# A decoder layer on one core: the values of two entries made by seven block products, with a new order of the slot

## The chip, the cores and the metric

The kernel runs on one core of a Trainium2 chip. The metric is the device time of one execution in microseconds (us), as the median of several runs.

## The reference, cut to what matters

One decoder layer on x of 16 entries, 128 tokens, 256 features, all float32: self attention with 16 heads of 64, cross attention with 16 heads of 16 to a context of the same size, and a feed-forward part of 8 experts with 512 hidden units each, all of them summed for every token. Each part adds to x after a layer norm. The change concerns the values of the self attention and their use:

```python
Q = jnp.einsum('btd,hkd->bthk', x, W_Q) + b_Q
K = jnp.einsum('btd,hkd->bthk', x, W_K) + b_K
V = jnp.einsum('btd,hkd->bthk', x, W_V) + b_V
attn = jax.nn.softmax(scores, axis=-1)
out_h = jnp.einsum('bhqs,bshk->bqhk', attn, V)
```

and the experts' first product, `einsum('nd,edh->neh', xf, w1)`, since a part of it is made early.

## The kernel before

The attention of the 16 entries runs in 16 slots, one for each entry. Slot s holds the self attention of entry s, the first steps of the cross attention of entry s-1 (its queries, scores and softmax) and the last ones of entry s-2, and it prepares later entries. After the slots comes a short tail, and then the experts, for 4 times 512 tokens.

**The order.** PE, DVE, ACT and POOL execute their instructions in the order in which the program gives them. Each step has a name and a due time in a table (DUE; FIRST_DUE and SECOND_DUE replace it for slots 0 and 1). `at` and `due` put a step on a heap at EXTRA + s x SLOT + DUE[name], and the steps are emitted in the order of these times. So only the order counts on the chip; a due time over SLOT falls into the next slot. Names that the prediction uses: S0, S1 (self scores, two halves of eight heads), max/ex/r/mul (softmax: DVE maximum, ACT exponentials of four heads with their sums, DVE reciprocal, POOL scaling; a c ahead means cross), T1 (transposes of the self weights on PE) and T2 (of the cross weights), each with a copy out of PSUM (a name that ends in e), SVa and SVb (self weights times values), SO and CO (output products, with xsSO and xsCO adding to x), bn, bn3 and root (variances and inverse roots of the two layer norms, on DVE), xn, xn3, LNx, LN3, LN1 (normalizing and transposing), CQ, CS, CV, ck, cvr (cross queries, scores, values, keys, value rows), q1x to qc0 and k1x to kc0 (queries and keys of two entries).

**Queries and keys** of a pair of entries are already made with seven block products in place of eight (`paired_steps`): `weight_sums` makes sums of weight blocks in slot 0, `pair_factors` makes four sums of token blocks of a pair (step tf), and each of the seven products is one of them times the other. What the products have in common is added outside PE: ACT copies (u0, c00), DVE adds (u1, u2, u3, c1, c0). One half of the columns of a pair is made in each slot, in four steps on PE (1x, 1y, 2x, 2y), and a later step adds to a PSUM bank that the adds have read before. The sums lie in `places`: sums_q (in a place of its own) and sums_k, which borrows the place w1_1 of a quarter of the experts' weights.

**Values** are made plainly (`values`, L604 on): one entry a slot, two halves of 512 columns, each two matmuls of 128x512 (128 deep, since 256 features are two blocks), and one ACT copy of 128x512 (ve0, ve1).

**Experts' weights ahead of time.** The first matmuls of the experts for tokens 0 to 511 are made already in slots 14 and 15 and in the tail (`pre_hidden`, L921 on; PRE_STEPS says at which step of those slots). Matmuls 0 to 7 need the first quarter of w1 (w1_0), the next eight the second (w1_1). SyncE's queue loads a quarter (1 MB) with one DMA (L242): w1_0 at the start of the kernel, w1_1 at S0 of slot 14, when sums_k is no longer read.

The tail's own PE and ACT instructions keep the order of the program too, but its DVE instructions do not: there the compiler's scheduler orders them by priority, and copies out of PSUM have a high one.

PSUM: scores use two double banks, and everything else in the slots rotates through four banks (`psum_mm`), so the fifth user waits until the first one's copies are done.

```python
a[1][0] = a[0][0] - a[1][0]   # combined(): the fourth of a weight's four sums, in place
nc.tensor.matmul(mm, tokens(b, k), wv[:, k, f], start=(k == 0), stop=(k == KD - 1))   # values
nc.tensor.matmul(mm, w1q[p // (NP // QN)][:, i, k, p % (NP // QN)], xnT[:, k, :MT], ...)   # pre_hidden
```

Of the kernel before, what the change touches and what calls it, by code (L numbers as in the profile page):

```python
# [48 lines left out]
NROW = 528  # L49


SLOT = 27.34
EXTRA = 7.5
DUE = dict(
    S0=0.0, S1=1.0, max0=1.2, LNx=2.0, LN3=2.22, max1=2.34, LNxc=2.42, cvr=2.44, LN3c=2.72,
    tf=3.0, ex0a=3.02, T2b1=3.31, T2b2=3.75, T2b1e=3.94, CQ=4.18, cvre=4.39, T2b2e=4.54,
    ex0b=4.74, T2a1=5.05, r0a=5.14, q2T=5.27, mul0a=5.42, T2a2=5.49, T2a1e=5.69, q1x=5.92,
    ex1a=6.11, T2a2e=6.28, xn1=6.5, q1y=6.82, r0b=6.88, mul0b=7.16, qu0=7.49, r1a=7.69, v1=7.72,
    ex1b=7.99, mul1a=8.19, qu1=8.21, qu2=8.64, qu3=9.07, LN1=9.44, r1b=9.56, ve1=9.64, q2x=9.66,
    st0=9.75, mid=9.77, late=9.77, st1=9.8, mul1b=9.84, LN1c=10.1, q2y=10.11, qc00=10.4,  # L60
    qc1=11.21, CS=11.23, qc0=11.56, msk0=12.38, T1a1=12.4, T1a2=12.84, ab1=13.0, T1a1e=13.03,
    T1b1=13.27, T1a2e=13.53, msk1=13.57, T1b2=13.71, T1b1e=14.03, CV=14.24, T1b2e=14.53,
    cmax0=14.76, SVa=15.29, at2T=15.9, cex0a=16.08, SVb=16.19, cmax1=16.24, CO=17.19,
    atT0=17.38, cex0b=17.45, atT1=17.98, k1x=18.05, cr0a=18.58, xsCO=18.71, cex1a=18.82,
    cmul0a=18.86, k1y=18.95, cr0b=19.05, bn3=19.18, SO=19.85, cmul0b=19.88, ku0=20.2, cr1a=20.4,
    cex1b=20.7, cmul1a=20.9, ku1=20.92, ku2=21.35, mid2=22.0, late2=22.0, ku3=22.03, cr1b=22.38,
    cmul1b=22.9, k2x=23.3, xsSO=23.5, k2y=23.75, bn=23.91, kc00=23.95, root=24.51, ck=24.65,
    v0=25.52, cke=25.72, kc1=26.86, kc0=27.21, ve0=27.44, xn=27.65, xn3=27.98, ab2=28.15,
)


# [9 lines left out]
    q1=17.2, atT1=17.21, q1e=17.6, k1=18.0, w1q=18.1, tf=18.2, SO=19.16, ke1=19.6, ws1=19.7,
    w1k=20.0, xsSO=22.81, bn=23.22, v1=23.47, root=24.79, xn=25.0, ck=25.2, ve1=25.39, q1x=26.9,
    qu0=26.95, cke=27.0, q1y=27.8, qu1=28.2, ab2=28.44, ab1=28.5, k1x=28.7, qu2=28.8, qu3=29.2,
    ku0=29.3, ku1=29.85, q2x=30.5, q2y=30.95, qc00=31.0, k1y=31.85, qc1=32.0, k2x=32.8,
    ku2=32.9, ku3=33.3, kc00=33.3, qc0=33.32, k2y=33.4, kc1=34.5, kc0=34.9,
)

SECOND_DUE = dict(xn1=2.9, ku0=18.7, st2=13.0, st3=22.4)

PRE_STEPS = (  # L90
    (14, "q1x", "qu1"), (14, "k1x", "kc00"),
    (15, "q1x", "qu1"), (15, "v1", "ve1"), (15, "k1x", "kc00"), (15, "v0", "ve0"),
)
ON_ACT = ('T1a', 'T1b')

EARLY = range(2, 6)
LATER = (("mid", range(6, 10), (1,), 2), ("late", range(10, B), (3, 4, 5), 6))
# [3 lines left out]
def decoder_layer(  # L101
# [53 lines left out]
    def psum_mm(name):  # L155
        return ps_mm.tile([P, 512], F32, tag="mm", name=name)
# [83 lines left out]
    def load_w1(i, pool):  # L240
        w = pool.tile([P, KD, E * F // QN], F32, tag=f"w1_{i}", name=f"w1_{i}")
        nc.sync.dma_start(out=w, in_=w1[:, :, i * E * F // QN : (i + 1) * E * F // QN])  # L242
        w1q[i] = w.rearrange("p k (q i c) -> p i k q c", i=2, c=P)

    def load_w2(i, pool):
# [1 line left out]
        nc.sync.dma_start(out=w, in_=w2[:, NF // QN * i : NF // QN * (i + 1), :])  # L247
        w2q[i] = w.rearrange("p (q j) (i c) -> p i j q c", j=2, c=P)

    load_w1(0, we1)  # L250

    places = (
        keep.tile([P, 4 * 512], F32, tag="k3", name="sums_q"),
        we1.tile([P, 4 * 512], F32, tag="w1_1", name="sums_k"),
    )


# [54 lines left out]
    def inverse_root(v, n, parts=None):  # L314

        y = small.tile([P, n], F32, tag=f"root{n}", name="root", bufs=6 if n < 3 else 1)
        t = small.tile([P, n], F32, tag=f"root_t{n}", name="root_t", bufs=2 if n < 3 else 1)
        nc.vector.tensor_scalar(t.bitcast(I32), v.bitcast(I32), 1, None, ALU.arith_shift_right)  # L320
# [23 lines left out]
    def variances(n):  # L344
        return small.tile([P, n, 2], F32, tag=f"mv{n}", name="mv", bufs=6 if n < 3 else 1)

    def statistics(mv, b):
        st = small.tile([P, 6], F32, tag="st", name="st")
# [3 lines left out]
    def inverse_deviations(mv, bs, parts=None):  # L352

        n = len(bs)
        v = small.tile([P, n], F32, tag=f"var{n}", name="var", bufs=6 if n < 3 else 1)
        nc.vector.tensor_scalar_add(v, mv[:, :, 1], LN_EPS)
        r = inverse_root(v, n, parts)
        return {b: (mv[:, i, 0:1], r[:, i : i + 1]) for i, b in enumerate(bs)}
# [172 lines left out]
        paired[x, n] = combined(a, more.rearrange("p (n q c) -> p n q c", n=3, c=P))  # L531

    def pair_factors(b0):
        t = places[b0 // 2 % 2][:, 1536:].rearrange("p (n t) -> p n t", n=4)
        x4 = [[tokens(b0 + i, k) for i in range(2)] for k in range(2)]
        paired[b0] = right(t, x4[0][0], x4[0][1], x4[1][0], x4[1][1])

    def paired_steps(x, b0, n):
# [26 lines left out]
        def first():  # L565
            v["a"], v["b"] = bank()
            product(1, v["a"], clears=True)
            product(6, v["b"])
            u = v["u"] = ap.tile([P, 2, 2, T], F32, tag="su", name="su")
            due(f"{x}u0", with_bias, u[:, 0], v["a"], 1)  # L570
            due(f"{x}u1", nc.vector.tensor_tensor, u[:, 0], u[:, 0], v["b"], ALU.add)

# [30 lines left out]

        return {f"{x}1x": first, f"{x}1y": second, f"{x}2x": third, f"{x}2y": fourth}  # L604

    def values(b, n, name="ve{}"):
        mm = psum_mm("mm_v")
        if ("v", b) not in entry:
            entry["v", b] = ap.tile([P, HD1], F32, tag="v", name="v")
        f = slice(n * 512, (n + 1) * 512)  # L610
        for k in range(KD):
            nc.tensor.matmul(  # L612
                mm,
                tokens(b, k),
                wv[:, k, f],
                start=(k == 0),
                stop=(k == KD - 1),
            )
        due(name.format(n), nc.scalar.copy, entry["v", b][:, f], mm)

    def self_scores(b, half):

# [19 lines left out]
    def self_values(b, half):  # L642


        if half == 0:
            entry["atT", b] = work.tile([P, C1, T], F32, tag="atT", name="atT")
        v, atT, prT = entry["v", b], entry["atT", b], entry["prT", b, half]
        po = psum_mm("po1").rearrange("p (c t) -> p c t", c=4)
        for c in range(4):
            for j in range(2):  # L650
                h = 2 * (4 * half + c) + j
# [31 lines left out]
    def cross_keys(b):  # L683
# [24 lines left out]

        due("cke", out)
        entry["k2T", b] = kT  # L710
        if i == GB - 1 and g + 2 < NG:
            contexts[g + 2] = context(g + 2)

    def cross_value_rows(b):
        g, i = b // GB, b % GB
        mm = psum_mm("mm_v2")
        for k in range(KD):
# [228 lines left out]
    def slot(s):  # L946
# [27 lines left out]
        if bs:  # L974
            at("LN1", self_norm_transposed, bs)
        b0 = s + 2 - s % 2
        if s % 2 == 0 and b0 < B:
            at("tf", pair_factors, b0)
# [470 lines left out]
```

## Time and profile before

| | |
|---|---|
| median of 3 runs | 858.74 us (858.65 to 858.94) |
| the profiled execution's own time | 858.52 us |
| its span, first to last instruction | 856.7 us |
| PE busy in the span | 847.0 us, 99% |
| DVE, ACT, POOL busy | 628.9, 462.3, 163.8 us |
| granted TensorE clock | 0.998 of full speed |
| slots 0 and 1 begin | 12.59 and 48.27 us |
| slots 2, 3, 4 begin | 74.13, 101.05, 128.54 us |
| slots 14, 15, tail begin | 400.90, 425.13, 449.28 us |

A slot is reckoned here from the first matmul of S0 to the next slot's. A busy share says little of PE: the trace models the ends of matmuls, and a matmul's record is longer than the time until the next one starts (593 ns against 430 ns for 128x512). So what an instruction costs PE is read from start to start, and that is done in the prediction. In rows with xN, N instructions in a row are merged; a float32 matmul stands as two instructions, a transpose as one. The DMA rows give the time from issue to landing.

### The profile page before, as it was taken

To read this page: it belongs to the slowest core of one execution; us is meant where nothing else is said; L and a number is where in the kernel's file an instruction comes from. 1 tells how busy PE (TensorE), PEld (TensorE's weight loads), DVE (VectorE), ACT (ScalarE), POOL (GpSimd) and SP (SyncE) were. 2 spreads that over 40 slices of the span, in tenths; PEclk is the share of its full clock that TensorE was granted. 3 is DMA by queue.
4 is the path that set the end of the run, shared out by engine and by line. 5 is a ranking of instruction groups with operands and counts; after the bars stand their busy time and mean duration, and the time that the engine had idled before them with its cause. 6 is when DMAs were issued, how large, how long until landed. Compare 5 with 4: busy or idle time off the path is not lost.

```text
span 856.7 us, 16095 instructions
## 1 busy us (share of the span) xinstructions
PE 847.0 (99%) x5850; PEld 704.6 (82%) x5850; DVE 628.9 (73%) x1651; ACT 462.3 (54%) x1688; POOL 163.8 (19%) x179
## 2 busy tenths in 40 slices
PE   8999999999999999999999999999999999999997
PEld 7888888888888888888775458888888888888886
DVE  5778888888787877878777497776566756575655
ACT  4567677676776767676674513343334343444342
POOL 5134243332424234242331000000000000000000
PEclk9999999999999999999999999999999999999999
DMA  8600000000000000001050100000000000000000
GB/s 240 195 2 14 2 6 10 2 13 1 2 14 2 14 2 2 14 2 50 11 217 21 49 1 1 0 13 14 1 1 0 25 1 2 0 13 13 1 1 25
DMA packets 18319, 21.30 MB, mean 25 GB/s; under 512 B 9584, under 2 KB 13696, under 8 KB 17600
## 3 DMA queue, kind: packets, MB, share of 16 engines
q1 hardware_dynamic: 17728, 19.93, 7.4%
q8 instruction: 46, 0.75, 0.3%
q0 software_dynamic: 368, 0.30, 0.1%
q14 instruction: 33, 0.27, 0.1%
q10 hardware_dynamic: 144, 0.04, 0.0%
HBM read 18.16 MB, written 2.10 MB: 24 GB/s over the span
## 4 chain that ended last, share of the span: by engine, by line
PE 94%; DVE 4%; ACT 1%; issue 1%; DMA 0%; DVEq 0%
PE y L1190 19%; PE mm_qk L550 10%; PE mm_o L672 6%; PE tr_p L428 6%; PE mm_v L612 6%; PE he L1190 5%; PE hf L1190 5%; PE ha L1190 5%; PE sc L628 4%; PE po L652 3%; PE mm_h L936 3%; PE y L1102 3%; PE hb L1190 3%; PE sc L762 2%; PE mm_o L821 2%; PE po L801 2%
## 5 line engine op out<-in xcount | busy, mean ns | idle before, releaser
L398 ACT ACTIVATE cpr<-sc,nmax 128x128 f32<-128x128 f32 x256 | 90.9, 407 | 16.0 <-DVE nmax L392 16.0
L398 ACT ACTIVATE pr<-sc,nmax 128x128 f32<-128x128 f32 x256 | 92.6, 429 | 2.7 <-DVE nmax L392 2.7
L413 POOL TENSOR_TENSOR cpr<-cpr,rinv 128x512 f32<-128x512 f32 x64 | 65.3, 1039 | 138.1 <-DVE rinv L409 113.9
L413 POOL TENSOR_TENSOR pr<-pr,rinv 128x512 f32<-128x512 f32 x64 | 65.7, 1039 | 87.2 <-DVE rinv L409 82.0
L1219 ACT ACTIVATE h<-u,colv 128x256 f32<-128x256 f32 x56 | 28.5, 508 | 93.9 <-DVE u L1206 92.0
L392 DVE TENSOR_REDUCE nmax<-sc 128x8 f32<-128x1024 f32 x64 | 76.5, 1217 | 1.3 <-PE sc L628 0.4
L1220 DVE TENSOR_TENSOR c<-u,hf 128x256 f32<-128x256 f32 x56 | 23.6, 421 | 69.3 <-PE hf L1190 69.1
L398 ACT ACTIVATION_READ_ACCUMULATOR pr<-sc,nmax 128x1 f32 x256 | 68.7, 268 | 0.0
L1190 PE MATMUL hf<-xt,w 128*128 128x256 f32 x224 | 66.9, 380 | 0.4 <-DVE u L1205 0.4
L1203 ACT COPY u<-ha 128x256 f32<-128x256 f32 x56 | 20.8, 372 | 85.0 <-PE ha L1190 85.0
L1190 PE MATMUL ha<-xnT,w 128*128 128x256 f32 x224 | 66.7, 379 | 0.0
L1190 PE MATMUL y<-t,w 128*128 128x256 f32 x224 | 66.7, 380 | 0.0
L398 ACT ACTIVATION_READ_ACCUMULATOR cpr<-sc,nmax 128x1 f32 x256 | 63.4, 248 | 0.0
L612 PE MATMUL mm_v<-wv,xnT 128*128 128x512 f32 x128 | 60.3, 594 | 0.0
L672 PE MATMUL mm_o<-wo,atT 128*128 128x256 f32 x256 | 58.0, 380 | 0.1
L1190 PE MATMUL y<-h,w 128*128 128x256 f32 x224 | 57.7, 380 | 0.0
L672 PEld LDWEIGHTS mm_o<-wo,atT 128*128 128x128 f32 x256 | 47.7, 191 | 7.0 <-DVE rinv L409 0.5
L1190 PEld LDWEIGHTS ha<-xnT,w 128*128 128x128 f32 x224 | 42.7, 190 | 7.0 <-issue 1.2
L1190 PEld LDWEIGHTS hf<-xt,w 128*128 128x128 f32 x224 | 42.5, 190 | 6.6 <-DVE u L1205 1.0
L310 ACT COPY prT<-tr_p 128x512 f32<-128x512 f32 x64 | 33.0, 603 | 26.8 <-PE tr_p L428 26.8
L1190 PEld LDWEIGHTS y<-h,w 128*128 128x128 f32 x224 | 42.7, 190 | 5.7
L1190 PEld LDWEIGHTS y<-t,w 128*128 128x128 f32 x224 | 42.0, 190 | 6.1 <-issue 0.8
(226 smaller groups left out, 1978.7 us busy)
## 6 DMA issues: line engine op xcount, KB each, us to landing
w<-in_w SPq DMA_DIRECT2D x8, 1024.0 KB, 5.2
ctx<-in_ctxT SPq DMA_DIRECT2D x8, 256.0 KB, 2.6
out_x<-ot SPq DMA_DIRECT2D x8, 256.0 KB, 2.2
xs<-in_x SPq DMA_DIRECT2D x3, 512.0 KB, 6.5
wk<-in_wk SPq DMA_DIRECT2D x2, 512.0 KB, 6.7
wq<-in_wq SPq DMA_DIRECT2D x2, 512.0 KB, 7.3
wv<-in_wv SPq DMA_DIRECT2D x2, 512.0 KB, 9.6
wo<-in_wo SPq DMA_DIRECT2D x1, 1024.0 KB, 8.5
```

The costliest lines, as they stand in the source:

```text
L310: f(*a)
L392: nc.vector.tensor_reduce(w["nmax"], sc, AX.X, ALU.max, negate=True)
L398: nc.scalar.activation(w["pr"][:, i, :], sc[:, i, :], AF.Exp, bias=w["nmax"][:, i : i + 1], scale=1.0, accum_out=sums[:, j : j + 1],)
L413: nc.gpsimd.tensor_tensor(four, four, w["rinv", n].unsqueeze(2).broadcast_to([P, 4, T]), ALU.mult)
L428: nc.tensor.transpose(tr[:, j, :], w["pr"][:, 4 * n + j, :], ident)
L550: nc.tensor.matmul(out[:, q, :], paired[x, n][m - 1][:, q], paired[b0][m - 1], start=clears and q == 0, stop=True, skip_group_check=True,)
L612: nc.tensor.matmul(mm, tokens(b, k), wv[:, k, f], start=(k == 0), stop=(k == KD - 1),)
L628: nc.tensor.matmul(sc[:, j, c * T : (c + 1) * T], qT[r, c, :], kT[r, c, :], start=True, stop=True,)
L652: nc.tensor.matmul(po[j * DH1 : (j + 1) * DH1, c, :], v[:, h * DH1 : (h + 1) * DH1], prT[:, 4 * j + c, :], start=True, stop=True,)
L672: nc.tensor.matmul(mm[:, :D], atT[:, c, :], wo[:, c, :], start=(c == 0), stop=(c == C1 - 1))
L1190: nc.tensor.matmul(out, left[p // q][n - 1][:, p % q], rights[n - 1], **flags)
L1219: nc.scalar.activation(h[:, 1, 1], u[:, 3], AF.Gelu, bias=col(B1 + 2 * p + 1))
```

## The change

1. Values. `paired_values` makes one half (512 columns) of the values of two entries a slot, with seven products of 128x256 in place of eight, from `pair_factors` of the pair and `value_sums` of wv (made in slots 0 and 1). Entries 0 and 1 are still made plainly, in slot 0. Pairs from entry 2 on are made in slots 1 to 14: half 0 of the pair b0 in slot b0 - 1, half 1 in slot b0. Copies and adds: vu0, vc00 on ACT; vu1, vu2, vu3, vc1, vc0 on DVE, all of 128x256.
2. Places. The value sums, sums_v, get the place w1_1, and sums_k moves to w1_0; `pair_factors` of pairs 2, 6, 10, 14 lie beside the value sums. The load of w1_0 moves from the start of the kernel to S0 of slot 14 (sums_k is last read by k2y of slot 13), and that of w1_1 to S0 of slot 15 (sums_v is last read by v2y of slot 14). Values lie in tiles of a pair and a half (`value_tile`).
3. T2a (transposes of half of the cross weights) is copied by ACT and no longer by DVE.
4. A new table DUE: ck, T2a ahead of the queries, the values v1x to v2y interleaved with q1x to q2y; LNx, cvr, T2b, CQ, CS, CV, CO later. SLOT is 26.98 (27.34 before). PRE_STEPS name other steps.

The diff, cut:

```diff
-SLOT = 27.34
-EXTRA = 7.5
+SLOT = 26.98
+EXTRA = 7.86
...
+    S0=0.0, S1=1.0, T2a1=2.05, T2a2=2.49, T2a1e=2.69, ck=2.92, T2a2e=3.19, max0=3.47, v1x=3.79,
+    cke=3.99, max1=4.61, v1y=4.66, vu0=5.19, q1x=5.52, ex0a=5.54, vu1=6.08, q1y=6.42, vu2=6.76,
+    qu0=6.91, r0a=7.11, vu3=7.24, v2x=7.32, mul0a=7.39, ex0b=7.41, qu1=7.63, v2y=7.77, qu2=8.06,
+    qu3=8.49, q2x=8.64, vc00=8.78, vc1=8.84, q2y=9.09, ex1a=9.13, vc0=9.19, r0b=9.53,
+    mul0b=9.81, LNx=9.99, qc1=10.19, cvr=10.21, qc00=10.51, qc0=10.54, r1a=10.98, LNxc=11.01,
+    T2b1=11.23, mul1a=11.26, cvre=11.31, ex1b=11.66, T2b2=11.66, T2b1e=11.86, CQ=12.1,
+    T2b2e=12.46, T1a1=12.97, q2T=13.17, T1a2=13.4, r1b=13.51, xn1=13.6, T1a1e=13.6, mul1b=13.79,
+    CS=13.93, st0=14.0, mid=14.0, late=14.0, T1a2e=14.1, ab1=14.9, CV=14.97, msk0=15.08,
+    LN3=16.07, at2T=16.27, T1b1=16.29, LN3c=16.49, msk1=16.61, T1b2=16.73, T1b1e=16.93,
+    LN1=17.16, T1b2e=17.43, SVa=17.47, cmax0=17.8, LN1c=17.93, SVb=18.38, tf=18.93, atT0=18.94,
+    cex0a=19.12, k1x=19.43, atT1=19.54, cmax1=20.14, k1y=20.33, cex0b=20.49, SO=21.23,
+    cr0a=21.28, cmul0a=21.56, ku0=21.86, cr0b=22.14, cex1a=22.36, cmul0b=22.58, ku1=22.58,
+    ku2=23.01, ku3=23.44, cex1b=23.74, cr1a=23.94, st1=24.0, mid2=24.0, late2=24.0, cmul1a=24.3,
+    k2x=24.68, xsSO=24.88, k2y=25.12, bn=25.28, kc00=25.32, cr1b=25.78, CO=26.03, cmul1b=26.06,
+    kc1=26.22, kc0=26.57, xsCO=27.09, bn3=27.5, root=28.09, xn=32.72, ab2=33.22, xn3=33.4,
...
-SECOND_DUE = dict(xn1=2.9, ku0=18.7, st2=13.0, st3=22.4)
+SECOND_DUE = dict(wv1=4.7, st0=11.9, st1=12.46, st2=16.3, st3=24.0)
...
-    (14, "q1x", "qu1"), (14, "k1x", "kc00"),
-    (15, "q1x", "qu1"), (15, "v1", "ve1"), (15, "k1x", "kc00"), (15, "v0", "ve0"),
+    (14, "q2x", "qc00"), (14, "k1x", "ku0"),
+    (15, "v1x", "vc00"), (15, "q1x", "qc1"), (15, "k1x", "ku0"), (15, "k2x", "kc00"),
...
-ON_ACT = ('T1a', 'T1b')
+ON_ACT = ('T1a', 'T1b', 'T2a')
...
-    load_w1(0, we1)
...
-        we1.tile([P, 4 * 512], F32, tag="w1_1", name="sums_k"),
+        we1.tile([P, 4 * 512], F32, tag="w1_0", name="sums_k"),
+        we1.tile([P, 4 * 512], F32, tag="w1_1", name="sums_v"),
...
-        t = places[b0 // 2 % 2][:, 1536:].rearrange("p (n t) -> p n t", n=4)
+        t = places[b0 % 4][:, 1536:].rearrange("p (n t) -> p n t", n=4)
...
+    def paired_values(b0, n):
...
+        def first():
+            v["a"], v["b"] = bank()
+            product(1, v["a"], clears=True)
+            product(6, v["b"])
+            u = v["u"] = ap.tile([P, 2, 256], F32, tag="su", name="sv", bufs=SU)
+            due("vu0", nc.scalar.copy, u[:, 0], v["a"])
+            plus("vu1", u[:, 0], u[:, 0], v["b"])
...
+            plus("vu2", u[:, 1], u[:, 0], v["f"])
+            plus("vu3", out[1][:, 1], u[:, 1], v["e"])
+
+        def third():
+            product(2, v["a"])
+            due("vc00", nc.scalar.copy, v["out"][0][:, 0], v["a"])
+
+        def fourth():
+            product(4, v["f"])
+            product(3, v["e"])
...
+            at("wv0", value_sums, 0)
+        elif b0 < B:
+            for name, f in paired_values(b0, 1 - s % 2).items():
+                at(name, f)
...
-        if s == B - 2:
-            at("S0", load_w1, 1, we1)
+        if s >= B - 2:
+            at("S0", load_w1, s - (B - 2), we1)
```

More of the change, by code (lines that the diff above doesn't have):

```diff
@@ L33 @@
 GT = GB * T
+SU = 2
 NP = NF // 2
@@ L49 @@
 NROW = 528
-SLOT = 27.34
-EXTRA = 7.5
+SLOT = 26.98
+EXTRA = 7.86
 DUE = dict(
[L55 to L68, printed above, removed]
@@ L80 @@
     T1b1e=12.74, LN1c=13.06, T1b2e=13.34, w0q=13.6, w0k=13.7, SVa=14.25, SVb=15.15, atT0=15.42,
[L81 to L85, printed above, removed]
+    q1=17.2, atT1=17.21, wv0=17.3, q1e=17.6, k1=18.0, w1q=18.1, tf=18.2, SO=19.16, ke1=19.6,
+    ws1=19.7, w1k=20.0, xsSO=22.81, bn=23.22, v1=23.47, root=24.79, xn=25.0, ck=25.2, ve1=25.39,
+    q1x=26.9, qu0=26.95, cke=27.0, q1y=27.8, qu1=28.2, ab2=28.44, ab1=28.5, k1x=28.7, qu2=28.8,
+    qu3=29.2, ku0=29.3, ku1=29.85, q2x=30.5, q2y=30.95, qc00=31.0, k1y=31.85, qc1=32.0,
+    k2x=32.8, ku2=32.9, ku3=33.3, kc00=33.3, qc0=33.32, k2y=33.4, kc1=34.5, kc0=34.9,
 )
-SECOND_DUE = dict(xn1=2.9, ku0=18.7, st2=13.0, st3=22.4)
+SECOND_DUE = dict(wv1=4.7, st0=11.9, st1=12.46, st2=16.3, st3=24.0)
 PRE_STEPS = (
-    (14, "q1x", "qu1"), (14, "k1x", "kc00"),
-    (15, "q1x", "qu1"), (15, "v1", "ve1"), (15, "k1x", "kc00"), (15, "v0", "ve0"),
+    (14, "q2x", "qc00"), (14, "k1x", "ku0"),
+    (15, "v1x", "vc00"), (15, "q1x", "qc1"), (15, "k1x", "ku0"), (15, "k2x", "kc00"),
 )
-ON_ACT = ('T1a', 'T1b')
+ON_ACT = ('T1a', 'T1b', 'T2a')
 EARLY = range(2, 6)
@@ L314, in inverse_root @@
     def inverse_root(v, n, parts=None):
-        y = small.tile([P, n], F32, tag=f"root{n}", name="root", bufs=6 if n < 3 else 1)
-        t = small.tile([P, n], F32, tag=f"root_t{n}", name="root_t", bufs=2 if n < 3 else 1)
+        y = small.tile([P, n], F32, tag=f"root{n}", name="root", bufs=6 if n < 3 else 2)
+        t = small.tile([P, n], F32, tag=f"root_t{n}", name="root_t", bufs=2)
         nc.vector.tensor_scalar(t.bitcast(I32), v.bitcast(I32), 1, None, ALU.arith_shift_right)
@@ L344, in variances @@
     def variances(n):
-        return small.tile([P, n, 2], F32, tag=f"mv{n}", name="mv", bufs=6 if n < 3 else 1)
+        return small.tile([P, n, 2], F32, tag=f"mv{n}", name="mv", bufs=6 if n < 3 else 2)
     def statistics(mv, b):
@@ L354, in inverse_deviations @@
         n = len(bs)
-        v = small.tile([P, n], F32, tag=f"var{n}", name="var", bufs=6 if n < 3 else 1)
+        v = small.tile([P, n], F32, tag=f"var{n}", name="var", bufs=6 if n < 3 else 2)
         nc.vector.tensor_scalar_add(v, mv[:, :, 1], LN_EPS)
@@ L568, in first @@
             product(6, v["b"])
-            u = v["u"] = ap.tile([P, 2, 2, T], F32, tag="su", name="su")
+            u = v["u"] = ap.tile([P, 2, 2, T], F32, tag="su", name="su", bufs=SU)
             due(f"{x}u0", with_bias, u[:, 0], v["a"], 1)
@@ L604, in paired_steps, with value_tile @@
         return {f"{x}1x": first, f"{x}1y": second, f"{x}2x": third, f"{x}2y": fourth}
+    def value_tile(b, n):
+        b -= b % 2
+        if ("v", b, n) not in entry:
+            if n == 0 and b % 4 == 0:
+                entry["v", b, n] = xnT[:, :, NT - 512 :]
+            else:
+                entry["v", b, n] = ap.tile([P, 2, 512], F32, tag=f"v{n}", name=f"v{n}", bufs=1)
+        return entry["v", b, n]
     def values(b, n, name="ve{}"):
         mm = psum_mm("mm_v")
-        if ("v", b) not in entry:
-            entry["v", b] = ap.tile([P, HD1], F32, tag="v", name="v")
         f = slice(n * 512, (n + 1) * 512)
@@ L618, in values, with value_sums, product, bank @@
             )
-        due(name.format(n), nc.scalar.copy, entry["v", b][:, f], mm)
+        due(name.format(n), nc.scalar.copy, value_tile(b, n)[:, b % 2, :], mm)
+    def value_sums(n):
+        a = wv[:, :, n * 512 : (n + 1) * 512].rearrange("p k (i c) -> p i k c", i=2)
+        more = places[2][:, n * 768 : (n + 1) * 768].rearrange("p (n c) -> p n c", n=3)
+        paired["v", n] = combined(a, more)
+    def paired_values(b0, n):
+        v = {}
+        def product(m, out, clears=False):
+            nc.tensor.matmul(
+                out, paired[b0][m - 1], paired["v", n][m - 1],
+                start=clears, stop=True, skip_group_check=True,
+            )
+        def bank():
+            t = psum_mm("mm_v").rearrange("p (o c) -> p o c", o=2)
+            return t[:, 0], t[:, 1]
+        def plus(name, *a):
+            due(name, nc.vector.tensor_tensor, *a, ALU.add)
+        def first():
[5 more added lines that the diff above has]
+            plus("vu1", u[:, 0], u[:, 0], v["b"])
+        def second():
+            v["f"], v["e"] = bank()
+            product(7, v["f"], clears=True)
+            product(5, v["e"])
+            t = value_tile(b0, n)
+            v["out"] = [t[:, i].rearrange("p (i c) -> p i c", i=2) for i in range(2)]
+            u, out = v["u"], v["out"]
+            plus("vu2", u[:, 1], u[:, 0], v["f"])
[6 more added lines that the diff above has]
+            product(3, v["e"])
+            u, out = v["u"], v["out"]
+            plus("vc1", out[0][:, 1], u[:, 0], v["f"])
+            plus("vc0", out[1][:, 0], u[:, 0], v["e"])
+        return {"v1x": first, "v1y": second, "v2x": third, "v2y": fourth}
     def self_scores(b, half):
@@ L646, in self_values @@
             entry["atT", b] = work.tile([P, C1, T], F32, tag="atT", name="atT")
-        v, atT, prT = entry["v", b], entry["atT", b], entry["prT", b, half]
+        v = value_tile(b, half)[:, b % 2]
+        atT, prT = entry["atT", b], entry["prT", b, half]
         po = psum_mm("po1").rearrange("p (c t) -> p c t", c=4)
@@ L650, in self_values @@
             for j in range(2):
-                h = 2 * (4 * half + c) + j
+                h = 2 * c + j
                 nc.tensor.matmul(
@@ L710, in cross_keys @@
         entry["k2T", b] = kT
-        if i == GB - 1 and g + 2 < NG:
-            contexts[g + 2] = context(g + 2)
     def cross_value_rows(b):
@@ L732, in cross_value_rows @@
         )
+        if i == GB - 1 and g + 2 < NG:
+            contexts[g + 2] = context(g + 2)
     def cross_queries(b):
@@ L976, in slot @@
         b0 = s + 2 - s % 2
-        if s % 2 == 0 and b0 < B:
-            at("tf", pair_factors, b0)
+        if s == 0:
+            at("tf", pair_factors, 2)
+        elif bs:
+            at("tf", pair_factors, bs[0])
         if b0 < B:
@@ L982, in slot @@
                     at(name, f)
-        if s + 1 < B:
+        b0 = s + s % 2
+        if s == 0:
             for n in range(2):
-                at(f"v{n}", values, s + 1, n)
-        if s == B - 2:
-            at("S0", load_w1, 1, we1)
+                at(f"v{n}", values, 1, n)
+            at("wv0", value_sums, 0)
+        elif b0 < B:
+            for name, f in paired_values(b0, 1 - s % 2).items():
+                at(name, f)
+        if s == 1:
+            at("wv1", value_sums, 1)
+        if s >= B - 2:
+            at("S0", load_w1, s - (B - 2), we1)
         for n, (s1, name, out) in enumerate(PRE_STEPS):
             if s1 == s:
-                copy = nc.vector.tensor_copy if out == "qu1" else nc.scalar.copy
+                copy = nc.vector.tensor_copy if out == "qc1" else nc.scalar.copy
                 at(name, pre_hidden, n, copy, out)
```

## The prediction

> **What bounds the kernel now.** I read the page first: the busy shares, and the chain of work that ended last.
>
> ```profile
> PE 847.0 (99%) x5850; PEld 704.6 (82%) x5850; DVE 628.9 (73%) x1651; ACT 462.3 (54%) x1688; POOL 163.8 (19%) x179
> ...
> PE 94%; DVE 4%; ACT 1%; issue 1%; DMA 0%; DVEq 0%
> ```
>
> The chain runs 94% through PE, so PE sets the time, and the question is whether it ever waits. I cut the span at the first matmul of S0 and asked for busy time by stretch (PE, PEld, DVE, ACT, POOL): slots 13, 14 and 15.
>
> ```profile
> 373.85:400.90 27.05, 27.05 (x253) 23.08 (x253) 21.48 (x55) 19.10 (x85) 9.02 (x9) 1.00 0.05 10
> 400.90:425.13 24.23, 24.23 (x205) 18.19 (x204) 17.54 (x40) 17.40 (x78) 9.01 (x9) 1.00 0.09 36
> 425.13:449.28 24.15, 24.15 (x206) 18.34 (x206) 17.73 (x44) 17.40 (x78) 9.02 (x9) 1.00 0.53 191
> ```
>
> PE has no idle time, at clock 1.00. Earlier slots of the steady part are alike: 27.05 us when even, 27.49 when odd (transposes LN1). So what leaves PE is gained, if the new order brings no waits. DVE is busy for 21.5 to 23.1 of 27.05. Slot 1 is the exception: 25.87 us from start to start, though its steps add up to 23.5 (27.05, less T2, CV, CO, LN3 3.96, plus LN1 0.44), so PE waits there for 2.3.
>
> **What the products save.** From the timeline of PE:
>
> ```profile
> 300.02 1.88 PE L612 MATMUL mm_v<-wv,xnT 128*128 128x512 f32 x4
> 301.74 0.61 PE L550 MATMUL mm_qk<-xnT,wq 128*128 128x128 f32 x4
> ...
> 311.80 3.62 PE L672 MATMUL mm_o<-wo,atT 128*128 128x256 f32 x16
> ...
> 315.26 0.61 PE L550 MATMUL mm_qk<-xnT,wk 128*128 128x128 f32 x4
> ```
>
> Start to start, four instructions of 512 columns cost 1.72 us, 0.430 each; sixteen of 256 columns cost 3.46, 0.216 each. Weight loads stay hidden at 256. A slot had two values of four instructions, 3.44 us; it gets 14 of 256 columns, 3.03. Saved: 0.42 us in each of 14 slots, 5.8 us.
>
> A rule speaks against this. The Trainium skill (TensorE: Matmul & The Clock Gate, Back-to-back issue gap) says that in streams of weight load and matmul the spacing follows both, some 81 ns at 128 columns and 131 at 512. An estimate for 256 by interpolating is 98: fourteen would cost 1.37 against eight's 1.05, so the change would lose 0.3 a slot, 4.5 in all. The rows show exact halving (0.216 to 0.430), so they decide.
>
> **What it adds in a steady slot.** DVE: five adds of 256 columns, less two copies of 512 (T2a). ACT: those two copies and two of 256, less two of 512. The busy sum is not the issue (DVE 23.1 + 5 x 0.34 - 2 x 0.65 = 23.5 of 26.9); the order is, since everything queues. Spacings are from these rows (a slot's timeline):
>
> ```profile
> 320.51 2.36 DVE L392 TENSOR_REDUCE nmax<-sc 128x8 f32<-128x1024 f32 x2
> ...
> 324.62 0.42 ACT L398 ACTIVATE pr<-sc,nmax 128x128 f32<-128x128 f32 x1
> ...
> 324.96 0.43 ACT L398 ACTIVATE pr<-sc,nmax 128x128 f32<-128x128 f32 x1
> ...
> 326.67 0.72 ACT L561 ACTIVATE su<-mm_qk,colv 128x128 f32<-128x128 f32 x2
> ...
> 327.17 0.48 ACT L398 ACTIVATE pr<-sc,nmax 128x128 f32<-128x128 f32 x1
> ...
> 342.95 0.42 DVE L310 TENSOR_TENSOR xs<-mm_o,xs 128x256 f32<-128x256 f32 x1 [0.94 <-PE mm_o L672]
> ...
> 344.09 0.17 DVE L356 TENSOR_SCALAR var<-mv 128x2 f32<-128x2 f32 x1
> ...
> 345.18 1.50 ACT L701 ACTIVATE k2T<-mm_k,bkp,par 128x128 f32<-128x128 f32 x4 [1.16 <-PE mm_k L689]
> ...
> 346.35 0.41 DVE L310 TENSOR_TENSOR kT<-su,mm_qk 128x256 f32<-128x256 f32 x1
> ```
>
> Read: an exponential takes 0.345 of ACT, two biased copies 0.50, four key copies 1.38; a maximum takes 1.15 of DVE, the add to x and the variance 1.14, the roots 2.26; a result of PE is used 0.20 after PE has moved on (its successor starts at 342.75).
>
> *First place, v2y*, which adds to a bank that vu3 must have read. Ahead of vu3 on DVE, after CO's end: 0.20, xsCO and bn3 1.14, root 2.26, two maxima 2.30, xn 0.32, vu1 0.34, xn3 0.32, vu2 0.34, r0a 0.10, vu3 0.42, handover 0.06: 7.80. PE in between: 0.09 of change-over to S0 (v0 took 1.81 to S0 here, not 1.72), scores 1.99, T2a 0.87, ck 0.89, v1 1.73, q1 1.79, v2x 0.43: 7.79. A tie: no wait, and no cover either.
>
> *Second place, T2b1*: it takes the bank of q1x, the fifth before it, so it waits for qc00. After ck, ACT has: 0.20, cke 1.38, vu0 0.26, ex0a 1.38, qu0 0.50, ex0b 1.38, vc00 0.26, ex1a 1.38, qc00 0.63, handover 0.06: 7.43. PE has v and q (3.03 + 3.13), LNx 0.22, cvr 0.87: 7.25. A wait of 0.18 in each slot; bounds 0 and 0.3, since both sums are of ten terms. I take 0.18, which the rows give. CQ, T1a, CS, SO and k2y come out with 0.2 us and more to spare. So a steady slot gains 0.24: slots 2 to 13 gain 2.9 us.
>
> **Ends of the stage.**
> - Slot 0: eight adds for the value sums, 1.6 us for each half. The first half falls between atT and qT, where DVE idled 1.04 and 0.70: nothing, and 0.7 if that cover is gone.
> - Slot 1: the second half's 1.6 comes after the maxima; vu3 ends at 6.9 from the slot's start, when PE reaches v2y at 6.9. CQ waits 0.35 for LNxc behind ex1a; SO waits 1.05 for atT0 behind two masks, cmax0 and tf. Sum 23.1 + 1.5 = 24.6 against 25.87: a gain of 1.2, bounds 0 and 1.6.
> - Slot 14 has no queries, so v2x follows v1y and v2y comes at 6.0 after CO, with vu3 still at 7.80: 1.8 lost, 0.4 saved, +1.4 (bounds 0.9 and 1.8).
> - Slot 15: the pre-product v1x is copied behind ex0a and ex0b, and T2b1 takes its bank: 0.5. CQ needs LNxc, which stands behind ex1a: done at 10.4, PE there at 9.7 with that wait: 0.75. Together +1.25 (bounds 0.5 and 1.6).
> - Load of w1_0: issued when k2y of slot 13 ends, 0.9 before CO ends; a load of 1 MB landed 5.2 us after issue, so 4.5 after CO, and pre-product 0 comes at 8.7: nothing. It would cost up to 5 if SyncE's queue stood still; only context loads are ahead, done by then. w1_1 follows v2y of slot 14; its first reader is in the tail.
> - Tail: here DVE copied T2, and its order is the scheduler's:
>
> ```profile
> 450.38 0.41 DVE L368 TENSOR_SCALAR xn<-xs,mv,root 128x256 f32<-128x256 f32 x1
> 450.71 2.48 DVE L290 COPY cprT<-tr_p 128x512 f32<-128x512 f32 x4
> 453.10 0.41 DVE L368 TENSOR_SCALAR xn<-xs,mv,root 128x256 f32<-128x256 f32 x1
> ```
>
> The copies overtook xn3, not the roots, and cost PE 0.6. With CO last in the slot, the roots stand 2.6 us later against T2. Two copies go to ACT (minus 0.6); the other two, if behind roots and xn, would stop CV of entry 14 for 2.2. Between -0.6 and +1.6, I take -0.2: two copies then find gaps, as copies overtook work here.
>
> Sum, against the profiled execution (858.52, of which 1.8 lies around the span): -2.9 - 1.2 + 1.4 + 1.25 - 0.2 = -1.7. On the median, 0.2 above it: 858.7 - 1.7 = 857.0.
>
> **Rivals.**
> - *ACT keeps up* (T2b1 does not wait): each steady slot gains all of 0.42, 2.2 more: 854.8. For it: one spacing 0.02 shorter in each of ten terms is enough. Against: the sum above.
> - *DVE becomes the bound at v2y*, the slower side. The tie of 7.80 to 7.79 has no slack, and each 0.1 by which the real chain is longer costs 1.2 over twelve slots; it decides from 0.3 on (860.6), and at 0.5 gives 863. For it: the chain starts at CO, the last step of the slot, and holds over twenty instructions in a row. Against: the terms are measured, and a statistic or reciprocal there takes 0.2.
> - *The ends lose more* (tail +1.6, slot 1 gains nothing): 857.0 + 1.8 + 1.2 = 860.0.
> - *The products do not get cheaper*, as the rule has it: some 867; excluded by the rows but for 2 in 100.
>
> **How the numbers follow.** Main case, 855.5 to 858.8: 0.50. ACT keeps up, 852.5 to 855.5: 0.22. Ends lose more, 858.8 to 860.4: 0.12. DVE bound or dearer products, over 860.4: 0.16. Within 0.2% is 857.0 to 860.5 (about what a measurement of this kernel can tell from no change), so the main case splits: half is below. Faster 0.25 + 0.22 = 0.47, the same 0.25 + 0.12 = 0.37, slower 0.16. The range 853.5 to 861.5 leaves out the best third of the second case and most of the last.
>
> **What would show it.** Value products 0.216 us apart. Steady slots at 26.8 (even) and 27.25 (odd), with the only regular PE gap before T2b1 and ACT su, qT as its releaser. A gap of 1.8 before v2y in slot 14, released by DVE; gaps before T2b1 and CQ in slot 15; no PE wait for a DMA in slot 14. I am wrong if v2y waits in each slot, if slots are at 26.6, or if PE waits in slot 14 for w.

## The result and the profile after

The changed kernel takes 862.76 us (median of 6 runs, 862.47 to 864.74), the kernel before 858.69 in the same series (858.56 to 858.94): a ratio of 1.0051, 95% interval 1.0038 to 1.0064. It is slower by 4 us, where I had forecast it faster by 1.7. The profiled execution took 862.73 us, with a span of 861.0 (856.7 before).

The busy shares and the chain of waits of the changed kernel:

```profile
PE 846.6 (98%) x5934; PEld 718.6 (83%) x5934; DVE 643.0 (75%) x1696; ACT 472.6 (55%) x1721; POOL 164.6 (19%) x179
...
PE 82%; DVE 13%; ACT 3%; issue 2%; DMA 1%; DVEq 0%; SPq 0%
```

PE's busy time is the same to 0.4 us, but the chain now leaves PE for 13% of the span to DVE and 3% to ACT (4% and 1% before): PE waits for them. Slots 13, 14 and 15, in the same columns as before:

```profile
375.11:402.11 27.00, 26.96 (x259) 23.99 (x259) 21.91 (x58) 19.62 (x87) 8.64 (x10) 1.00 0.01 2
402.11:428.09 25.98, 24.36 (x212) 19.21 (x211) 17.72 (x45) 18.64 (x81) 8.46 (x9) 1.00 0.25 82
428.09:453.62 25.53, 24.59 (x205) 18.31 (x205) 16.86 (x44) 18.47 (x80) 10.15 (x11) 1.00 0.50 179
```

The clock is full, and PE has 1.6 and 0.9 us of idle time in the last two slots. The ledger of both traces, slot by slot (us, first score matmul of S0 to the next slot's; the tail is reckoned from the first T2 behind slot 15 to the end of the span):

| | before | after | difference | forecast |
|---|---|---|---|---|
| start of slot 0 | 12.59 | 12.84 | +0.25 | 0 |
| slot 0 | 35.68 | 35.67 | -0.01 | 0 |
| slot 1 | 25.87 | 24.60 | -1.27 | -1.2 |
| slots 3 and 7 | 27.49 each | 29.00, 28.79 | +2.81 | -0.48 |
| the other ten of 2 to 13 | most 27.05 or 27.49 | most 27.00 or 27.44 | -0.56 | -2.4 |
| slot 14 | 24.23 | 25.98 | +1.75 | +1.4 |
| slot 15 | 24.15 | 25.53 | +1.38 | +1.25 |
| tail and experts | 407.46 | 407.33 | -0.13 | -0.2 |

The sum is +4.2, which is the difference of the spans before they are rounded. The start differs by more than this from execution to execution (12.6 to 14.7 in the traces below), so its 0.25 means nothing. Two rows hold most of what went wrong: slots 3 and 7, and the ten plain slots, each with 0.06 gained instead of 0.24.

**A plain slot.** PE in slot 8 (start us, us, engine, line, operation, tiles), where q1 ends and v2x, v2y follow; then DVE and POOL in the same stretch:

```profile
246.50 0.60 PE L642 MATMUL mm_v<-wv,xnT 128*128 128x256 f32 x2
247.15 0.70 PE L642 MATMUL mm_v<-wv,sums_q 128*128 128x256 f32 x2
247.68 0.59 PE L642 MATMUL mm_v<-sums_v,xnT 128*128 128x256 f32 x2
248.11 0.61 PE L551 MATMUL mm_qk<-xnT,wq 128*128 128x128 f32 x4
```

```profile
245.27 0.41 DVE L311 TENSOR_TENSOR sv<-sv,mm_v 128x256 f32<-128x256 f32 x1
245.60 0.71 DVE L369 TENSOR_SCALAR xn<-xs,mv,root 128x256 f32<-128x256 f32 x1
246.23 0.41 DVE L311 TENSOR_TENSOR sv<-sv,mm_v 128x256 f32<-128x256 f32 x1
246.56 0.17 DVE L410 RECIPROCAL rinv<-sums 128x4 f32<-128x4 f32 x1
246.67 0.42 DVE L311 TENSOR_TENSOR v<-sv,mm_v 128x256 f32<-128x256 f32 x1
```

```profile
245.43 0.72 POOL L382 TENSOR_TENSOR xs<-xs,rowv 128x256 f32<-128x256 f32 x1 [6.05 <-DVE xn L369]
```

A product of 128x256 (two instructions) takes 0.43 from start to start (247.68 to 248.11): 0.216 an instruction, as forecast. But v2y's first product comes at 247.15, 0.65 after v2x instead of 0.43. It waits for vu3, the fifth DVE row, which ends at 247.09. And after a wait the next instruction is late too: 0.53 to 247.68. So v2y loses 0.22 + 0.10. On DVE, xn3 (second row) takes 0.71 us. It ends at 246.31, just after POOL's ab2 does (245.43 + 0.72 = 246.15): it was held. In the kernel before, no instruction of this line took more than 0.42. The shortest, median and longest in ns, before and after:

```profile
L368 DVE TENSOR_SCALAR xn<-xs,mv,root x48: 403/409/417, 5.6 to 488.6; 128x256 f32<-128x256 f32 x48
L369 DVE TENSOR_SCALAR xn<-xs,mv,root x48: 382/411/1134, 5.7 to 492.4; 128x256 f32<-128x256 f32 x48
```

**Slot 3.** At the end of slot 2 DVE has six small root instructions (mid2) ahead of xsSO. Here are the first three, POOL's scaling in the same stretch, and xsSO:

```profile
97.86 0.13 DVE L334 TENSOR_TENSOR root_t<-root 128x4 f32<-128x4 f32 x1
98.03 0.17 DVE L335 TENSOR_TENSOR root_t<-root_t,var 128x4 f32<-128x4 f32 x1
98.23 0.95 DVE L336 SCALAR_TENSOR_TENSOR root<-root_t,root 128x4 f32<-128x4 f32 x1
...
98.12 1.04 POOL L414 TENSOR_TENSOR cpr<-cpr,rinv 128x512 f32<-128x512 f32 x1 [0.73 <-DVE root_t L334]
...
99.68 0.42 DVE L311 TENSOR_TENSOR xs<-mm_o,xs 128x256 f32<-128x256 f32 x1
```

One of them takes 0.95 where its equals take 0.16: it started after POOL's scaling (98.12 to 99.16) and ended with it. The six take 1.82 from the first one's start to xsSO, and the chain to vu1 and vu3 starts 1.60 later than in slot 8 (xsCO 1.71 after the slot's start, not 0.11). PE shows it in slot 3:

```profile
108.04 0.70 PE L642 MATMUL mm_v<-wv,xnT 128*128 128x256 f32 x2 [0.66 <-DVE sv L311]
109.44 0.48 PE L642 MATMUL mm_v<-wv,sums_q 128*128 128x256 f32 x1 [0.71 <-DVE xnT L311]
```

### The profile page after: what moved, and what is told of

Same layout as the page of the kernel before. It is cut to its first block, busy times and chain, and to the rows that moved or that the text cites. A ratio compares the mean times of both kernels' runs of the same rounds, so it can differ in the third digit from the quotient of the medians.

```text
span 861.0 us, 16374 instructions
## 1 busy us (share of the span) xinstructions
PE 846.6 (98%) x5934; PEld 718.6 (83%) x5934; DVE 643.0 (75%) x1696; ACT 472.6 (55%) x1721; POOL 164.6 (19%) x179
## 4 chain that ended last, share of the span: by engine, by line
PE 82%; DVE 13%; ACT 3%; issue 2%; DMA 1%; DVEq 0%; SPq 0%
PE y L1264 19%; PE mm_qk L551 8%; PE he L1264 5%; PE hf L1264 5%; PE ha L1264 5%; PE mm_o L737 5%; PE tr_p L429 5%; PE mm_v L642 3%; PE y L1176 3%; PE mm_h L1001 3%; PE po L717 3%; PE hb L1264 3%; DVE nmax L393 3%; PE sc L692 2%; PE mm_qk L486 2%
## 5 line engine op out<-in xcount | busy, mean ns | idle before, releaser
L399 ACT ACTIVATION_READ_ACCUMULATOR pr<-sc,nmax 128x1 f32 x256 | 65.8, 257 | 0.0
L311 DVE COPY_PREDICATED_SCALAR sc<-hidden_keys,masked 128x1024 f32 x30 | 38.4, 1279 | 9.6 <-PE sc L827 9.3
L382 POOL TENSOR_TENSOR xs<-xs,rowv 128x256 f32<-128x256 f32 x32 | 23.4, 742 | 103.7 <-DVE xn L369 103.7
```

Source lines behind the costliest of these rows:

```text
L311: f(*a)
L399: nc.scalar.activation(w["pr"][:, i, :], sc[:, i, :], AF.Exp, bias=w["nmax"][:, i : i + 1], scale=1.0, accum_out=sums[:, j : j + 1],)
```

## The experiments

**Theory 1:** the loss is a DVE chain lengthened by POOL: ab2 against xn3 in each slot, and the root steps against POOL's scaling in slots 2 and 6. **Theory 2:** several chains end nearly together in the new order, so that removing one only hands the wait to the next.

**1. ab2_late**, on the changed kernel: `ab2=33.22` to `ab2=34.5`, behind xn3.

> The changed kernel with one due time other: ab2 (POOL's add of a bias to x) at 34.5 and no longer at 33.22, so that it starts behind mul0a and not between xn and xn3. Theory 1 (POOL holds up xn3): xn3 takes 0.41 us and not 0.71, v2y no longer waits 0.2 to 0.3, steady slots fall from 27.00 and 27.44 to about 26.75 and 27.2; with slots 3 and 7 some 0.3 shorter too, the time is 862.7 - 12 x 0.25 = 859.7. Theory 2 (DVE's chain ahead of vu3 is too long by its own number of instructions): xn3 may get shorter, but v2y waits as before; 862.5 to 862.9.

Measured: 861.74 us (ratio to before 1.0029, 1.0019 to 1.0039). Xn3 is back at 0.41 and v2y's wait falls to 0.07 (with 0.10 behind it; r0a, just ahead of vu3, now waits 0.13 for ACT's exponentials), but the plain slots stay at 27.02 and 27.46. PE in slot 8:

```profile
248.05 0.66 PE L551 MATMUL mm_qk<-sums_v,wq 128*128 128x128 f32 x4
...
249.22 1.03 PE L781 MATMUL mm_v<-wx_vo,ctx 128*128 128x256 f32 x4
250.20 1.06 PE L429 MATMUL tr_p<-ident,cpr 128*128 128x128 f32 x8
```

From cvr (L781) to T2b1 (L429) it is 0.98, not 0.87: T2b1 now waits for ACT, whose copy qc00 ends at 250.10. The hold is real, but it hid another wait of nearly the same length. Most of the 1 us gained is in slots 3 and 7 (28.71 and 28.50) and slot 14 (25.79).

**2. mid2_early**, on the changed kernel: `mid2=24.0, late2=24.0` to `20.3` each.

> The changed kernel with the second steps of the two long inverse roots (mid2 in slot 2, late2 in slot 6) at 20.3 in place of 24.0, ahead of cr0a and of POOL's cmul0a, and out of the run of DVE work from xsSO to vu3. Theory 1 (these six instructions, stretched by POOL to some 1.9 us, make DVE late for vu3 of slots 3 and 7): slots 3 and 7 fall from 29.00 and 28.79 to 27.5, the time by 2.8 to 859.9. Theory 2 (slots 3 and 7 are long because their values go to the place in xnT, or from some other work of these slots): they stay at 28.8 to 29.0, 862.7.

Measured: 860.05 us (1.0007, 0.9997 to 1.0017). Slots 3 and 7 are 27.49 and 27.44, nothing else moves. The root steps' place cost 2.7 us.

**3. both_moved**, edits 1 and 2 together.

> Both moves of due times together. Theory 1 (two separate causes, both DVE's lateness at vu3): the gains add up, 862.7 - 3.0 - 2.8 = 856.9, which is also the sum of the prediction. Theory 2 (one slack serves both, so that the second move finds nothing left or another wait takes over): 858.5 to 860.

Measured: 859.97 us (1.0007, 0.9997 to 1.0016), no better than edit 2 alone. So ab2 against xn3 costs nothing in the plain slots while T2b1 waits behind it: theory 2 there. T2b1 starts 11.37 to 11.39 after the start of slot 8 in the changed kernel and in experiments 1 and 3 alike, although v2y's first product is 0.13 to 0.14 earlier in the last two.

**4. plain_values**, the changed kernel's order and places, with the values made plainly again; the value sums and DVE's value adds are left out:

```diff
-            at("wv0", value_sums, 0)
...
-            for name, f in paired_values(b0, 1 - s % 2).items():
-                at(name, f)
+            for i, (name, out) in enumerate((("v1x", "vu0"), ("v2x", "vc00"))):
+                at(name, values, b0 + i, 1 - s % 2, out)
...
-            at("wv1", value_sums, 1)
```

> The changed kernel with the values of each pair made plainly: at step v1x two matmuls of 512 columns for the first entry, at v2x two for the second, one ACT copy of 512 each; the value sums and the five adds a slot on DVE are left out, the rest of the order stays. So PE has 0.42 us a slot more and DVE 1.7 less. Theory 1 (DVE's lateness at v2y costs the change what the products save): nothing waits for vu3 any more, so slots 3 and 7 are like their neighbours and slot 14 loses its wait of 1.9; 862.7 + 5.8 - 3.6 - 2.8 - 1.9 = 860.2, so the products as placed here cost 2.5. Theory 2 (the new order of the slot itself is the dear part): waits stay elsewhere and the time is over 866.

Measured: 868.03 us (1.0099, 1.0084 to 1.0114). The slots are 27.64 and 28.07, with waits of 0.25 + 0.10 in q2 and 0.20 before T2b1. Against it the products save 5.3 us. With the plain values' PE work this order is some 9 us slower than the kernel before, about 0.6 in each plain slot. The root steps' place is hardly any of it: slots 3 and 7 take 28.28 and 28.07, and slots 5 and 9 take 28.09 and 28.07, since nothing waits for a vu3 here. Nor do the 9 us say what the order costs the products: ACT's copies of plain values are of 512 columns and take 0.48 from start to start at v1x, where vu0 takes 0.25, and the 0.23 that this adds is about as long as the wait in q2.

**5. qc00_first**, edits 1 and 2 and `qc00=10.51` to `9.12`, ahead of ex1a on ACT.

> Base: both_moved (small root steps moved ahead and ab2 moved behind xn3, 860.0 us, steady slots 27.0 and 27.44). One more edit: the copy qc00 stands ahead of the exponentials ex1a on ACT, so that the bank that T2b1 takes comes free 1.4 us earlier. Theory: after both moves the only thing that holds PE in a steady slot is ACT's chain from ck to qc00, so T2b1 stops waiting, the slots fall to 26.75 and 27.2, and the kernel takes about 857. Rival: the time a slot has over its streams is not one wait but the switches between steps plus whichever of several chains is late next (ex1a and ex1b are now 0.6 later, so cross scores or T1b1 wait); the slots stay at 27.0 and 27.44 and the time at 860.

Measured: 858.80 us (0.9997, 0.9988 to 1.0006). Plain slots fall by 0.14 to 26.86 and 27.30: T2b1's wait is gone (it was 0.07 to 0.12, with 0.03 behind it). Theory right on the place and half right on the size: what remains is v2y's 0.06 + 0.10 and 0.05 to 0.10 in q2y. Slot 14 pays for it: it rises from 25.78 to 26.43, since CQ there now waits 0.55 for LNxc, which stands behind ex1a.

**6. edges**, edits 1 and 2, and pre-products of the experts where PE waits:

```diff
-    (14, "q2x", "qc00"), (14, "k1x", "ku0"),
-    (15, "v1x", "vc00"), (15, "q1x", "qc1"), (15, "k1x", "ku0"), (15, "k2x", "kc00"),
+    (14, "q1x", "qu0"), (14, "k1x", "ku0"),
+    (15, "v1x", "vc00"), (15, "q1x", "qc1"), (15, "q2x", "qc00"), (15, "k1x", "ku0"),
```

> Base: both_moved (860.0 us, slot 14 25.78, slot 15 25.53). The pre-products of the experts are put where PE waits in the last two slots: in slot 14 the first stands at q1x, ahead of v2x, in place of q2x behind it; in slot 15 a third one stands at q2x, ahead of T2b1 and CQ, in place of k2x. Theory: those slots lose time in waits (for the adds behind the maxima, and for the copies behind the exponentials) that a product of 0.86 us fills; slot 14 falls by 0.9 to 1.7, slot 15 by 0.6 to 1.2, and the kernel takes 857 to 858.5. Rival: a pre-product's own copy goes into the same ACT queue and its own result into the same banks, so it delays what PE is waiting for by as much as it fills; slots 14 and 15 stay within 0.3, and the time at 859.7 to 860.

Measured: 858.09 us (0.9985, 0.9976 to 0.9994). Slot 14 falls from 25.78 to 24.85, slot 15 from 25.53 to 24.49, and the tail takes 0.45 longer. PE in slot 14 at the values' second part, in the changed kernel and then with this edit:

```profile
408.72 0.70 PE L642 MATMUL mm_v<-wv,xnT 128*128 128x256 f32 x2 [0.91 <-DVE sv L311]
410.13 0.70 PE L642 MATMUL mm_v<-wv,sums_v 128*128 128x256 f32 x2 [0.71 <-DVE v L311]
```

```profile
404.81 1.88 PE L1001 MATMUL mm_h<-xnT,w 128*128 128x512 f32 x4
406.53 0.59 PE L642 MATMUL mm_v<-wv,xnT 128*128 128x256 f32 x2
407.10 0.70 PE L642 MATMUL mm_v<-wv,sums_v 128*128 128x256 f32 x2
```

The pre-product (L1001) stands in the gap. The theory holds, in slot 14 at the lower end of its numbers: CQ now waits 0.67 for LNxc there, with 0.10 behind it, and the tail pays 0.45.

**7. t2a_dve**, the changed kernel with `ON_ACT = ('T1a', 'T1b')`: T2a copied by DVE again.

> Base: the changed kernel (862.76). T2a is copied by DVE again, as before the change; everything else stays. This tells what part 3 of the change is worth. Theory: DVE's chain from CO to vu3 is as long as PE's way to v2y, so two copies of 0.65 in it cost PE 1.2 us in each of twelve slots, and ACT's relief brings nothing: about 875. Rival: DVE had slack ahead of the maxima (they wait for the scores anyway) and it is ACT's chain that holds T2b1; then the slots stay or fall by 0.2 and the time is 860 to 863.

Measured: 879.88 us (1.0240, 1.0221 to 1.0258). Plain slots are 28.15 and 28.59, 1.15 longer; slots 3 and 7 are 30.2. The waits are at v2x and v2y (0.43 and 0.87, each with 0.10 behind it). Nearly all of the two copies' time on DVE (1.19 from the first one's start to the maximum behind them) reaches PE: DVE's chain to vu3 has no slack, so part 3 is a condition for the rest.

**8. best**, all four edits.

> All four edits on the changed kernel: small root steps ahead, ab2 behind xn3, qc00 ahead of ex1a, pre-products into the gaps of slots 14 and 15. If both theories of this batch hold, 3 us come off from the steady slots and 2.9 from the last two, off 860.0: about 854, which is under the kernel before. If only the last slots' theory holds: about 857. If neither: 860.

Measured: 857.02 us (0.9975, 0.9963 to 0.9986): faster than both kernels. The slots are 26.86 and 27.30, slot 14 is 24.84; both gains of experiments 5 and 6 are there, less than the 854 that I expected of the whole, since 5 gave half in the plain slots and 6 two thirds.

**9. xn3_late**, experiment 8 and `xn3=33.4` to `38.03`, far behind vu3.

> Base: the run with all four edits (857.02 us; steady slots 26.86 and 27.3; v2y's fourth product still 0.065 late behind vu3, the one after it 0.10 late, q2y 0.05 to 0.1). One more edit: xn3 goes from ahead of vu3 to 4 us behind it on DVE; LN3, its reader, is another 5 us later. Theory: v2y's bank is still held by DVE's chain from the output product to vu3, which gets 0.4 us shorter; v2y no longer waits, the slots fall by 0.17 to 26.7 and 27.15, and the kernel takes 855.0. Rival: the rest is no wait but what a switch to the value products costs; the slots and the time stay (856.8 to 857.2).

Measured: 856.78 us (0.9979, 0.9970 to 0.9987); slots 26.87 and 27.31. The wait at v2y stays (0.07 + 0.10), though DVE's chain has lost an instruction. DVE says why:

```profile
161.19 0.18 DVE L410 RECIPROCAL rinv<-sums 128x4 f32<-128x4 f32 x1 [0.27 <-ACT pr L399]
161.28 0.39 DVE L311 TENSOR_TENSOR v<-sv,mm_v 128x256 f32<-128x256 f32 x1
```

The reciprocal r0a stands ahead of vu3 and waits 0.27 for ACT's exponentials ex0a. My rival (a switch to value products costs that) was wrong too: it is a wait, by another way.

**10. r0a_late**, experiment 9 and `r0a=7.11` to `7.3`, behind vu3.

> Base: the run with xn3 behind vu3 (856.78; steady slots 26.87 and 27.31). There DVE stands 0.27 us in front of the reciprocal r0a, which waits for ACT's exponentials ex0a, and vu3 is queued behind it, so that v2y is as late as before. One more edit: r0a goes behind vu3. Theory: vu3 comes 0.35 earlier, v2y no longer waits (0.07 and the 0.10 of the instruction after it), the slots fall to 26.7 and 27.15, and the kernel takes 854.8. Rival: with v2y free, the next late chain (ACT's copies before q2y or T2b1) takes it over, as it did twice; slots and time stay (856.6 to 856.9).

Measured: 856.67 us (0.9975, 0.9966 to 0.9984); slots 26.86 and 27.30. PE in slot 5:

```profile
163.16 0.60 PE L642 MATMUL mm_v<-wv,xnT 128*128 128x256 f32 x2
163.59 0.59 PE L642 MATMUL mm_v<-wv,sums_v 128*128 128x256 f32 x2
164.03 0.59 PE L642 MATMUL mm_v<-sums_v,xnT 128*128 128x256 f32 x2
164.46 0.61 PE L551 MATMUL mm_qk<-xnT,wq 128*128 128x128 f32 x4
165.02 0.71 PE L551 MATMUL mm_qk<-sums_v,wq 128*128 128x128 f32 x4
165.57 0.61 PE L551 MATMUL mm_qk<-xnT,sums_q 128*128 128x128 f32 x4
```

V2 runs without a gap for the first time, and q2y, two steps on, is late by 0.12 and 0.10 (0.56 and 0.55 instead of 0.45). The rival holds. It also closes the account: 27.05 - 0.42 + 0.22 = 26.85, and 26.86 was measured. The products save all of 0.42; the rest is q2y's wait and what follows it.

**11. before_ab2**, on the kernel before: `ab2=28.15` to `27.8`, ahead of xn3 in the program.

> Base: the kernel before (858.77 us), with nothing of the change in it. One edit: POOL's addition ab2 is put just ahead of xn3 on DVE, as it stands in the changed kernel. Theory: xn3 is held while POOL's instruction runs, so it takes 0.7 us or more in place of 0.41, whatever the values' products are; it costs nothing here or 0.1 a slot, since no step of PE is near behind it (858.7 to 860). Rival: the longer xn3 of the changed kernel comes from the value adds around it; then xn3 stays at 0.41 here.

Measured: 858.66 us (1.0005, 0.9995 to 1.0014), xn3 0.41. Inconclusive: ab2 waits for xn, and xn3 follows xn directly on DVE, so ab2 still started 0.17 after xn3. The edit did not make the case.

**12. before_apart**, on the kernel before: `xn=27.65` to `27.0`, so that kc0 stands between xn and xn3.

> Base: the kernel before (858.62), with nothing of the change in it. One edit: xn stands ahead of the last key copy kc0 on DVE, so that another DVE instruction comes between xn and xn3, as vu1 does in the changed kernel; ab2 on POOL follows xn and then starts ahead of xn3. Theory: xn3 is held until POOL's instruction ends and takes 0.6 to 0.8 us in place of 0.41, in most steady slots; the time stays within 1 us, since DVE has slack there. Rival: the longer xn3 of the changed kernel comes from the value adds around it; then xn3 stays at 0.41 here.

Measured: 858.77 us (1.0000, 0.9991 to 1.0009). DVE, then POOL:

```profile
237.90 0.41 DVE L368 TENSOR_SCALAR xn<-xs,mv,root 128x256 f32<-128x256 f32 x1
238.23 0.60 DVE L597 SCALAR_TENSOR_TENSOR kT<-mm_qk,bqk,su 128x128 f32<-128x128 f32 x2
238.75 0.52 DVE L368 TENSOR_SCALAR xn<-xs,mv,root 128x256 f32<-128x256 f32 x1
```

```profile
238.39 0.73 POOL L381 TENSOR_TENSOR xs<-xs,rowv 128x256 f32<-128x256 f32 x1 [4.03 <-DVE xn L368]
```

Xn3 is held until ab2 ends at 239.12 and takes 0.52 (0.6 was my lower bound, as only the last 0.37 of ab2 lay against it). The hold needs nothing of the change but an instruction between xn and xn3: there it was vu1.

## Why the prediction was wrong, point by point

- *What the products save*: right. 0.216 an instruction and 0.42 a slot, as experiment 10 shows; the stream figures of the Trainium skill (TensorE: Matmul & The Clock Gate, Back-to-back issue gap), from which the prediction had estimated 0.098, do not fit here.
- *What the change moves*: the step that failed most. I costed the products, the adds and T2a, but not the small root steps mid2 and late2, whose due time went from 22.0 to 24.0, into the chain from SO over xsSO and CO to vu3. Slots 3 and 7 cost 2.81 instead of gaining 0.48 (experiment 2 takes back 2.7).
- *First place, v2y, "a tie: no wait"*: wrong by 0.3 a slot. Four terms were off. "xn3 0.32" took 0.63 from start to start, held by ab2 (experiments 1, 12). "r0a 0.10" was counted as DVE work, though it waits for ACT, so without the hold v2y still waits 0.07 (experiments 1 and 9). The instruction after one that waited came 0.10 late, which no sum of mine had. And T2a took 0.93 on PE, not 0.87, which covers a little. In slot 8 DVE's chain from CO's end was 8.06 instead of 7.80, PE's way 7.84 instead of 7.79: 0.22 of wait. The rival that DVE becomes the bound at v2y had the place and the sign.
- *Second place, T2b1, "a wait of 0.18"*: the mechanism was right, but I took it as the only wait, and it was too small: from ck's end to T2b1's start ACT's chain took 7.56 (slot 8 of the changed kernel and of experiments 1 and 3), not 7.43, so that alone it would have cost 0.31 by the 7.25 of PE. In the changed kernel next to nothing of it is left to see (0.01), and 0.07 to 0.12 once v2y is less late (experiments 1, 3): waits in a row on one engine don't add up, as a late v2y gives ACT the time that T2b1 would wait for.
- Together the ten plain slots gained 0.56 instead of 2.4. Of the 0.37 by which one misses 0.42, v2y holds 0.32 in slot 8 and T2b1 0.04 (0.01 ahead of it and 0.03 behind); in slot 5, which gained nothing (27.49 and 27.50), v2y holds 0.31 and q2y 0.10.
- *Ends*: slot 1 right in its sum (-1.27), in part by luck: SO waited 0.57, with 0.10 behind it, and not 1.05, and several lots of 0.1 that I had not counted made up for it. Slots 14 and 15 were right in place and cause and short by 0.35 and 0.13. The load of w1_0 was hidden. T2's tail copies found gaps between the roots as said, and were worth more than said: from the first T2 to CV PE takes 3.56, and took 4.08 before. Most of that is lost again at the very end: from the last matmul's start the span runs on for 4.93 instead of 4.53. No run tells why.
- The error of 5.9 in the sum of the spans: slots 3 and 7 3.3, the ten slots 1.8, the ends and the tail 0.5, the start 0.25.

What stays open: whether q2y's last 0.22 can be freed. Its product is late behind a DVE add that waits for ACT's copy qu0; no further order was tried.

## What to carry to other kernels

List every step whose place in the order moves, however small, and ask what it now stands in front of; six small instructions, five of 0.16 us and one that POOL stretched to 0.95, made more than half of the loss here. A sum that ends in a tie isn't "no wait": look in each chain for an instruction that waits on another engine, and treat two near ties as one budget, since freeing one hands the wait to the other. A saving of PE time is worth only what the second and third latest chains allow, and that is measured by removing them one after another.

## What the runs showed of the hardware

- DVE's tensor_scalar of 128x256 from SBUF to SBUF was held about to the end of a POOL instruction that had started before it: xn3 0.41 to 0.71 in the changed kernel, xn1 in some slots up to 1.13. So was a root step with two inputs in SBUF, of 128x4, from 0.16 to 0.95. Not every instruction from SBUF to SBUF was: in the changed kernel batch_norm_stats kept to its 0.43 (21 times) and a reciprocal to its 0.18 (19 times) when they started while POOL ran, and adds that read PSUM stayed at 0.41 to 0.42. When xn3 started first, POOL's addition was the longer one (0.83, against 0.73 when it came first). The Trainium skill (SBUF — State Buffer, Who interferes with whom) states it: DVE and POOL share a pair of SBUF ports, whichever issues first holds it for its whole instruction, and tensor_scalar can need the pair, as can a form with two inputs in SBUF while POOL reads there. The trace agrees, and I had not applied it.
- After a float32 product that waited for another engine, the next instruction started 0.10 late, whatever the length of the wait (0.06 in experiment 5, 0.22 in the changed kernel, 0.87 in experiment 7): a wait has a fixed price on top. After T2b1, a transpose, it was 0.03 (experiments 1 and 3). The trace suggests that the price is a weight load: in experiment 1 the waiting product and its load both start at 246.64, while the instruction at 246.35 had its load started at 246.13. No run tests that.
